# A hybrid transformer block on one core: the last feed-forward part in halves, identity products in planned waits, a first load by tiles, and new constants in the planner that orders the work

## The chip, the cores and the metric

The kernel runs on one core of one Trainium2 chip. A core has TensorE (PE: matrix products and transposes, results into eight PSUM banks), VectorE (DVE), ScalarE (ACT), GpSimd (POOL), the DMA engines, and SyncE (SP), which here issues most DMAs. The metric is the device time of one execution in microseconds (us). Before the change the median of three runs is 2589.13 us (2588.81 to 2591.01).

## The reference

The input is 16 sequences of 512 tokens by 256 channels, float32. Each sequence goes through four residual stages, each on its layer-normed input, called a, f, b and h in the kernel:

```
x = x + attn_a(norm(x))   # a: 16 heads of 16; keys within 32 tokens, or one of the
                          #    first 4 tokens as key or query; softmax; out projection
x = x + ffn(norm(x))      # f: 256 -> 768 twice, silu(gate) * up, 768 -> 256, int weights / 127
x = x + attn_b(norm(x))   # b: exp(rotated q.k) / sum(exp(unrotated q.k)), causal mask after
                          #    the division, times v; out projection
x = x + ffn(norm(x))      # h: the same weights as f
```

In b the denominator runs over all 512 keys, also those that the causal mask takes out of the numerator.

## The kernel before, in words

All weights lie in SBUF. A sequence `b` (0 to 15) is held as four tiles of 128 tokens (`xt`, tile index `t`), and its stages are Python generators that yield one operation at a time: `normalize` (L460), `window_attention` (a), `feed_forward` (f and h, L1032), `rotary_attention` (b), `products` (L1289), `load` and `store`. Per stage one sequence is in work at a time; different stages work on different sequences at once, so in steady state a of one sequence runs beside f, b and h of earlier ones.

The order of the instructions on every engine is written by a planner, `Plan` (L86), before the kernel is emitted. Every yielded operation carries an engine, an estimated time, the names that it needs, and the buffers that it takes and gives back. `Plan.run` repeatedly takes, from the operations that could start soonest, the one of lowest key, and emits it there; each engine executes its own list in that order, and semaphores hold an instruction until its inputs are there. The plan is made once.

On TensorE the key is the rank of the thread and then `progress` plus `turn`. Progress is the number of the sequence, plus a fixed lead of the stage (`LEAD`: a 0, f 0.885, b 1.59, h 2.77), plus the share of the stage that is done: it sets how far apart the stages run. `turn` is a price for changing the shape in which the 128x128 array is used. There are three shapes: FULL (all rows and columns; transposes, and in the profile `128*128`), COLS (four column strips of 32, `128*32`) and ROWS (four row strips of 32, the score products `dn`, `nm` and `sa`, `32*128` and `32*64`). Projections are FLEX: FULL when the array is in FULL, otherwise COLS. `TURN` has the price of each change, in sequences, and `hold`, the time for which an operation in ROWS is awaited when the array is in ROWS. On the other engines the key is: operations that give a buffer back first, then rank, then progress.

Names for the trace: `lt_*` are the transposes of a normed input, `xnt_*` the transposed copies, `psc_g*`/`psc_u*` gate and up products, `th_*` the tanh and silu product, `ht_*` the hidden layer, `po_*` a projection back to 256 channels. In a: `sa` scores, `sc` masked scores and weights, `tp` their transposes, `ya` the products with the values. In b: `dn` scores of the denominator, whose exponentials ACT sums (L1164); `nm` rotated scores, whose exponentials go to `ptb` (L1215), where POOL zeroes what is above the diagonal (L1225); `yb` the products with the values (L1309); `db` the inverse denominators, by which DVE multiplies `yb` (L1319).

`products` runs over ten groups, five for each half of the channels (`oc`), and sums a half's five groups in one bank; only after the fifth does DVE read the bank, for all 512 tokens. A half's third and fourth group end what tokens 0 to 255 need; the fifth holds keys 256 to 383 alone. The projection of b follows in four tiles of tokens, and each adds its result to `xt` (L547). `normalize` of stage h then takes statistics by tile (L471, L472), the inverse deviation of all four tiles at once on POOL (L475, L476), scales four tiles (L481) and transposes them; both halves of the transposed channels are copied out (L517, L519), and only then does the first gate product run. `xn` has one buffer, `ht` and the transposed input of f and h (`in_f`) one each.

The loads are issued at the top: sequence 0 in one DMA of 512 KB on SP (L273), then on the same queue `wk`, `wq`, `wv`, `wo` (L319), sequence 1, the three raw feed-forward weights (L330), `wqkv` and `wout`. `make_identity` writes the identity matrix `ident` with POOL.

Of the kernel before, what the change touches and what calls it, by code (L numbers as in the profile page):

```python
# [81 lines left out]
LAG = {"pe": 0.26, "act": 0.2, "dve": 0.2, "pool": 0.2, "sp": 0.1}  # L82
BORDER = {"fr": 0.30, "fc": 0.15, "rf": 0.21, "rc": 0.13, "cf": 0.21, "cr": 0.21}
NEVER = 1e9

class Plan:  # L86
# [3 lines left out]
    def __init__(self, slots):  # L90
        self.free = dict.fromkeys(LAG, 0.0)
        self.at = {}
        self.slots = {tag: [0.0] * n for tag, n in slots.items()}
        self.threads = []
        self.lying = FULL
        self.slow = 0.0
        self.sbuf = 0.0
        self.done = {}

# [3 lines left out]
    def ready(self, op):  # L103
# [3 lines left out]
        for tag in op.takes:  # L107
            if tag in ("u", "s"):
                at = max(at, sorted(self.slots["bank"])[0 if tag == "u" else 3])
            if tag != "s":  # L110
                at = max(at, min(self.slots[tag]))
# [8 lines left out]
    def take(self, op):  # L120

        for tag in op.takes:
            if tag == "s":
                op.k[tag] = [self.pick("bank") for _ in range(4)]
            elif tag == "u":
                op.k[tag] = self.pick(tag), self.pick("bank")
            else:
                op.k[tag] = self.pick(tag)
# [8 lines left out]
    def progress(self, thread):  # L137

        _, _, stage, seq, _ = thread
        return seq + LEAD[stage] + self.done.get((stage, seq), 0.0) / SHARE[stage]  # L140
# [14 lines left out]
    def run(self):  # L155
        while True:
# [4 lines left out]
            for t in self.threads:  # L161
# [9 lines left out]
                cand.append((start, t))  # L171
            assert cand, [(t[2], t[3], t[1].needs, t[1].takes) for t in self.threads]
# [17 lines left out]
            else:  # L190
                start, t = min(soon, key=lambda c: (not c[1][1].gives, c[1][4], self.progress(c[1])))
            op = t[1]
            us = op.us
            if engine == "pe":
                op.lying = self.lies(op)
# [26 lines left out]
TURN = {"hold": 0.05, "fr": 0.0, "fc": 0.3, "rf": 0.3, "cf": 1.0, "rc": 0.0, "cr": 0.15}  # L222
LEAD = {"a": 0.0, "f": 0.885, "b": 1.59, "h": 2.77}
# [3 lines left out]
def kernel(  # L227
# [43 lines left out]
    def load_x(b, k):  # L271
        t = work.tile([P, NT, D], F32, tag=f"x{k}", name=f"x_{b}")
        nc.sync.dma_start(t, x[b].rearrange("(t p) d -> p t d", p=P))  # L273
# [185 lines left out]

    def normalize(stage, b):  # L460

        me = f"{stage}{b}"
        needs = added(before[stage], b) if stage in before else [f"x{b}"] * NT
        slot = input_of[stage]
        for t in range(NT):
            op = yield dve(0, needs[t], us=0.51)
            if t == 0:
                xt = xs[b]
                stats = work.tile([P, NT, 6], F32, tag=f"stats_{stage}", name=f"stats_{me}")
                mv = work.tile([P, NT, 2], F32, tag=f"mv_{stage}", name=f"mv_{me}")  # L470
            nc.vector.bn_stats(stats[:, t, :], xt[:, t, :])  # L471
            nc.vector.bn_aggr(mv[:, t, :], stats[:, t, :])  # L472
        op = yield pool(0, op.end, us=1.6)
        rstd = work.tile([P, NT], F32, tag=f"rstd_{stage}", name=f"rstd_{me}")
        nc.gpsimd.tensor_scalar(rstd, mv[:, :, 1], EPS, None, ALU.add)  # L475
        nc.gpsimd.tensor_tensor(rstd, rstd, neg_half, ALU.pow)  # L476
        op = yield dve(0, op.end, us=1.5, takes=("xn", slot), sbuf=True)
        k_xn = op.k["xn"]
        xn = work.tile([P, NT, D], F32, tag="xn", name=f"xn_{me}")
        for t in range(NT):  # L480
            nc.vector.tensor_scalar(  # L481
                xn[:, t, :],
                xt[:, t, :],
                mv[:, t, 0:1],
                rstd[:, t : t + 1],
                ALU.subtract,
                ALU.mult,
            )
        there = op.end
        if stage in "ab":  # L490
            bias = bias_sb["bo" if stage == "a" else "bout"]

            def add_bias(op):
                nc.gpsimd.tensor_tensor(
                    xt, xt, bias.unsqueeze(1).to_broadcast([P, NT, D]), ALU.add
                )

            plan.start(
                one(pool(0, there, "bo", us=2.3, makes=f"bias_{me}", sbuf=True), add_bias), stage, b, 2
            )  # L500
        else:
            plan.at[f"bias_{me}"] = 0.0
        for c in range(NC):
            op = yield pe(
                0.44, there, takes=("u",), gives=(("xn", k_xn),) if c == NC - 1 else ()
            )
            ps = bank(op, [P, S], f"lt_{me}_{c}")
            for t in range(NT):
                nc.tensor.transpose(
                    ps[:, t * P : (t + 1) * P], xn[:, t, c * P : (c + 1) * P], ident  # L510
                )
            if c == 0:
                xnt[me] = work.tile([P, NC, S], F32, tag=slot, name=f"xnt_{me}")

            def keep(_, c=c, ps=ps):
                if c == 0:
                    nc.vector.tensor_copy(xnt[me][:, c, :], ps)  # L517
                else:
                    nc.scalar.copy(xnt[me][:, c, :], ps)  # L519

            how = dict(gives=(("u", op.k["u"]),), makes=f"xnt_{me}.{c}")
            plan.start(
                one(dve(S, op.end, **how) if c == 0 else act(S, op.end, **how), keep), stage, b, -1
            )
# [952 lines left out]
```

## Time and profile before

| | |
|---|---|
| median of three runs | 2589.13 us |
| the profiled execution | 2590.64 us |
| its span, first to last instruction | 2588.8 us |
| PE busy | 2540.2 us, 98% |
| DVE / ACT / POOL busy | 1560.9 / 1479.0 / 947.8 us |
| chain that ended last | PE 94%, DVE 2%, ACT 2% |
| mean granted TensorE clock | 0.993 |

The profile tells of one execution. Busy times are shares of the span; 40 digits cut the span into equal slices and give the busy share of an engine in tenths, and PEclk the TensorE clock that was granted, in tenths of full speed. A row of the timeline gives the start, the time, engine, line, operation, what it writes and reads, the shape, the count, and in brackets the idle time before it with what ended that. A row of the table by stretches gives, for a stretch of the span, the busy time and instructions of each engine, then the granted clock, the share of DMA time and GB/s.

### The profile page before, as it was taken

To read this page: it belongs to the slowest core of one execution; us is meant where nothing else is said; L and a number is where in the kernel's file an instruction comes from. 1 tells how busy PE (TensorE), PEld (TensorE's weight loads), DVE (VectorE), ACT (ScalarE), POOL (GpSimd) and SP (SyncE) were. 2 spreads that over 40 slices of the span, in tenths; PEclk is the share of its full clock that TensorE was granted. 3 is DMA by queue.
4 is the path that set the end of the run, shared out by engine and by line. 5 is a ranking of instruction groups with operands and counts; after the bars stand their busy time and mean duration, and the time that the engine had idled before them with its cause. 6 is when DMAs were issued, how large, how long until landed. Compare 5 with 4: busy or idle time off the path is not lost.

```text
span 2588.8 us, 79000 instructions
## 1 busy us (share of the span) xinstructions
PE 2540.2 (98%) x34928; PEld 1266.8 (49%) x34928; DVE 1560.9 (60%) x3046; ACT 1479.0 (57%) x3689; POOL 947.8 (37%) x963
## 2 busy tenths in 40 slices
PE   7899999999999999999999999999999999999998
PEld 4554445455454544545445453554545445454434
DVE  7854856557574665746558565575746657465332
ACT  3646574746647465474755647455474654647473
POOL 5612524144351533424244341443515344241201
PEclk9899999999999999999999999999999999999999
DMA  4100010000100001000000100001000010100000
GB/s 140 26 24 2 2 41 2 25 18 2 41 2 25 19 2 41 2 25 18 19 24 2 41 2 24 19 2 41 2 25 18 2 41 2 33 2 2 10 10 9
DMA packets 26680, 50.81 MB, mean 20 GB/s; under 512 B 2337, under 2 KB 21217, under 8 KB 26337
## 3 DMA queue, kind: packets, MB, share of 16 engines
q1 hardware_dynamic: 24976, 44.83, 6.1%
q8 instruction: 274, 4.49, 0.7%
q10 hardware_dynamic: 1360, 0.93, 0.1%
q14 instruction: 70, 0.57, 0.1%
HBM read 13.77 MB, written 8.39 MB: 9 GB/s over the span
## 4 chain that ended last, share of the span: by engine, by line
PE 94%; DVE 2%; ACT 2%; DMA 1%; POOL 1%; issue 0%; SPq 0%; POOLq 0%; ACTq 0%; DVEq 0%
PE dn L1183 11%; PE psc_gh L451 7%; PE nm L1249 7%; PE po_h L451 7%; PE psc_uh L451 7%; PE psc_uf L451 7%; PE psc_gf L451 6%; PE po_f L451 6%; PE yb L1309 5%; PE tp L866 4%; PE sa L737 3%; PE ya L924 2%; PE po_a L451 2%; PE psc_qb L451 2%; PE po_b L451 2%; PE psv_b L451 2%
## 5 line engine op out<-in xcount | busy, mean ns | idle before, releaser
L1164 ACT ACTIVATE dn<-dn 128x512 f32<-128x512 f32 x1024 | 599.4, 585 | 146.5 <-PE dn L1183 146.5
L1215 ACT ACTIVATE ptb<-nm 128x512 f32<-128x512 f32 x640 | 330.0, 606 | 276.0 <-PE nm L1249 275.9
L1183 PE MATMUL dn<-kt,qb 32*128 32x512 f32 x2048 | 302.7, 638 | 0.0
L1225 POOL TENSOR_SCALAR_AFFINE_SELECT ptb<-ptb 128x512 f32<-128x512 f32 x256 | 159.3, 634 | 384.7 <-ACT ptb L1215 384.7
L818 POOL TENSOR_TENSOR sc<-sc,sm 128x1056 f32<-128x1056 f32 x128 | 249.1, 1952 | 114.7 <-DVE sm L813 66.0
L803 POOL TENSOR_TENSOR sc<-sc,sm 128x1056 f32<-128x1056 f32 x120 | 232.6, 1952 | 140.8 <-DVE sm L785 129.3
L1164 ACT ACTIVATION_READ_ACCUMULATOR dn<-dn 128x1 f32 x1024 | 192.0, 187 | 0.0
L772 DVE TENSOR_TENSOR sc<-sa,mask 128x512 f32<-128x512 f32 x256 | 159.7, 680 | 51.1 <-PE sa L737 51.1
L1249 PE MATMUL nm<-qr,kr 32*128 32x512 f32 (+3 forms) x2048 | 189.6, 462 | 0.7 <-DVE sc L772 0.7
L451 PE MATMUL psc_gh<-xnt_h,wg_sb 128*32 128x512 f32 (+1 forms) x1452 | 189.4, 596 | 0.0
L1044 ACT ACTIVATE th_f<-psc_gf 128x512 f32<-128x512 f32 x96 | 57.8, 602 | 230.2 <-PE psc_gf L451 230.2
L451 PE MATMUL psc_uh<-xnt_h,wu_sb 128*32 128x512 f32 (+1 forms) x1308 | 183.4, 595 | 0.0
L451 PE MATMUL psc_uf<-xnt_f,wu_sb 128*32 128x512 f32 (+1 forms) x1476 | 183.1, 594 | 0.0
L451 PE MATMUL psc_gf<-xnt_f,wg_sb 128*32 128x512 f32 (+1 forms) x1476 | 182.8, 593 | 0.0
L451 PE MATMUL po_h<-wd_sb,ht_h 128*32 128x256 f32 (+1 forms) x1992 | 178.1, 381 | 0.2 <-ACT sc L810 0.2
L451 PE MATMUL po_f<-wd_sb,ht_f 128*32 128x256 f32 (+1 forms) x2856 | 177.7, 380 | 0.0
L1183 PEld LDWEIGHTS dn<-kt,qb 32*128 32x128 f32 x2048 | 87.8, 183 | 179.3 <-ACT dn L1164 76.0
L1309 PE MATMUL yb<-ptb,vb 128*32 128x512 f32 (+3 forms) x2048 | 169.7, 441 | 1.0 <-POOL ptb L1225 1.0
L812 DVE TENSOR_REDUCE sm<-sc 128x8 f32<-128x1056 f32 x120 | 148.3, 1236 | 19.4 <-ACT sc L810 19.2
L785 DVE TENSOR_REDUCE sm<-sc 128x8 f32<-128x1056 f32 x128 | 154.6, 1238 | 0.0
L601 POOL COPY rdcb<-rden 128x1024 f32<-128x1024 f32 x16 | 16.6, 1036 | 352.6 <-DVE rden L1264 352.6
L810 ACT ACTIVATE sc<-sc 128x1056 f32<-128x1056 f32 x120 | 128.8, 1090 | 29.2 <-POOL sc L803 27.4
(175 smaller groups left out, 4087.8 us busy)
## 6 DMA issues: line engine op xcount, KB each, us to landing
vw<-va SPq DMA_DIRECT2D x30, 576.0 KB, 5.5
x<-in_x_dram SPq DMA_DIRECT2D x16, 512.0 KB, 3.9
out_dram<-x SPq DMA_DIRECT2D x16, 512.0 KB, 3.0
vw<-va SPq DMA_DIRECT2D x30, 144.0 KB, 5.4
vw<-vb SPq DMA_DIRECT2D x2, 576.0 KB, 6.1
raw_wg_sb<-in_w_gate_dram SPq DMA_DIRECT2D x1, 768.0 KB, 8.9
raw_wu_sb<-in_w_up_dram SPq DMA_DIRECT2D x1, 768.0 KB, 10.3
raw_wd_sb<-in_w_down_dram SPq DMA_DIRECT2D x1, 768.0 KB, 11.4
```

The costliest lines, as they stand in the source:

```text
L451: nc.tensor.matmul(out[s], w[:, s], moving, skip_group_check=True, **how)
L772: nc.vector.tensor_tensor(flat[:, 4 * j : 4 * j + 4, 0:P], ps[j].rearrange("p c two w -> p (c two) w"), mask.unsqueeze(1).to_broadcast([P, ...
L785: nc.vector.tensor_reduce(small[:, 0, hs], part, AX.X, ALU.max, negate=True)
L803: nc.gpsimd.tensor_tensor(part, part, small[:, 0, hs].unsqueeze(2).to_broadcast([P, H // 2, P + NG]), ALU.add,)
L812: nc.vector.tensor_reduce(small[:, 1, hs], part, AX.X, ALU.add)
L818: nc.gpsimd.tensor_tensor(part, part, small[:, 1, hs].unsqueeze(2).to_broadcast([P, H // 2, P + NG]), ALU.mult,)
L1164: nc.scalar.activation(ps[j], ps[j], AF.Exp, scale=SCALE, accum_out=den[:, t, h : h + 1])
L1183: nc.tensor.matmul(ps[j], tiles["qb"][rows, par, oc, t * P : (t + 1) * P], tiles["kt"][rows, oc, :], start=True, stop=True,)
L1215: nc.scalar.activation(pt[:, j, :], ps[j], AF.Exp, scale=SCALE)
L1225: nc.gpsimd.affine_select(out=pt[:, :, at : at + P], in_=pt[:, :, at : at + P], pattern=[[0, 4], [1, P]], compare_op=ALU.is_ge, fill=0.0, ...
L1249: nc.tensor.matmul(ps[j][:, at : at + n], tiles["kr"][rows, oc, c * P : (c + 1) * P], tiles["qr"][rows, par, oc, c * P :], start=True, sto ...
L1309: nc.tensor.matmul(y_ps[rows, c * P :], vb[:, c, 4 * oc + j, par : par + 2, :], pt[:, j, at : at + n], start=len(seen) == 1, stop=len(seen ...
```

## The change

There are five parts.

1. Stage h of sequence 15 works in two halves of 256 tokens: norm, transposes, gate, up and down projections of tokens 0 to 255, then the same of tokens 256 to 511. For this, the second half of the channels of `products` of sequence 15 is summed in two banks, one for each half of the tokens; the first is read after the fourth group, the second after the fifth. `xn` and the inverse deviations are made for each half.
2. Where the planner expects TensorE to wait over 1.2 us (`FILL`), and a bank is free by then, it emits products of `ident` with `ident` (128x128, FULL) ahead of the waiting operation: (gap - 0.35) / 0.22 of them; for the very first wait (gap - 5) / 2 stands for the gap. The array counts as FULL afterwards. Their results are not read.
3. Sequence 0 is loaded in four DMAs of 128 KB, one for each tile of tokens, and its statistics wait for their own tile in the plan.
4. In the plan's first 110 us (`EARLY`), the engines other than TensorE take the lowest sequence first, ahead of the old key. A POOL operation that shares the SBUF port (`sbuf`) is planned after a VectorE one that could start at about the same time.
5. The constants are others: `TURN` (hold 0.05 to 0.15; FULL to COLS 0.3 to 0.15; ROWS to FULL 0.3 to 0.2; COLS to FULL 1.0 to 0.2; ROWS to COLS 0 to 0.05; COLS to ROWS 0.15 to 0.05), `LEAD` (f 0.727, b 1.333, h 2.645), and `ENDS`, which moves seven single stages of the first and last sequences.

```diff
+FILL = 1.2
+EARLY = {"us": 110.0}
...
             for tag in op.takes:
-            if tag in ("u", "s"):
-                at = max(at, sorted(self.slots["bank"])[0 if tag == "u" else 3])
+            n = {"uu": 2, "s": 4}.get(tag, 1)
+            if tag in ("u", "uu", "s"):
+                at = max(at, sorted(self.slots["bank"])[n - 1])
...
-        return seq + LEAD[stage] + self.done.get((stage, seq), 0.0) / SHARE[stage]
+        return seq + LEAD[stage] + ENDS.get(f"{stage}{seq}", 0.0) + self.done.get((stage, seq), 0.0) / SHARE[stage]
...
+            first = [c[0] for c in cand if c[1][1].sbuf and c[1][1].engine == "dve"]
+            if first:
+                least, us = min((c[0], c[1][1].us) for c in cand if c[1][1].sbuf and c[1][1].engine == "dve")
+                cand = [
+                    (least + us, t) if t[1].sbuf and t[1].engine == "pool" and least <= s <= least + us else (s, t)
+                    for s, t in cand
+                ]
...
-                start, t = min(soon, key=lambda c: (not c[1][1].gives, c[1][4], self.progress(c[1])))
+                start, t = min(
+                    soon,
+                    key=lambda c: (
+                        c[1][3] if least < EARLY["us"] else 0,
+                        not c[1][1].gives,
+                        c[1][4],
+                        self.progress(c[1]),
+                    ),
+                )
             op = t[1]
             us = op.us
             if engine == "pe":
+                gap = start - self.free["pe"]
+                if not self.free["pe"]:
+                    gap = (gap - 5.0) / 2
+                k = min(range(8), key=lambda k: self.slots["bank"][k])
+                if gap > FILL and self.fill and self.slots["bank"][k] <= self.free["pe"]:
+                    self.fill(k, int((gap - 0.35) / 0.22))
+                    self.lying = FULL
+                    self.free["pe"] = start
...
-TURN = {"hold": 0.05, "fr": 0.0, "fc": 0.3, "rf": 0.3, "cf": 1.0, "rc": 0.0, "cr": 0.15}
-LEAD = {"a": 0.0, "f": 0.885, "b": 1.59, "h": 2.77}
+TURN = {"hold": 0.15, "fr": 0, "fc": 0.15, "rf": 0.2, "cf": 0.2, "rc": 0.05, "cr": 0.05}
+LEAD = {"a": 0.0, "f": 0.727, "b": 1.333, "h": 2.645}
+ENDS = {"b0": -0.05, "b2": -0.29, "h0": -0.04, "a0": 0.57, "a1": -0.08, "f15": -0.26, "h13": -0.11}
...
-        nc.sync.dma_start(t, x[b].rearrange("(t p) d -> p t d", p=P))
+        src = x[b].rearrange("(t p) d -> p t d", p=P)
+        for part in [slice(i, i + 1) for i in range(NT)] if b == 0 else [slice(NT)]:
+            nc.sync.dma_start(t[:, part, :], src[:, part, :])
...
+    def parts_of(stage, b):
+        n = 2 if stage == "h" and b == B - 1 else 1
+        return [slice(S // n * i, S // n * (i + 1)) for i in range(n)]
...
...     # normalize: all of it inside
+        for n, tokens in enumerate(parts_of(stage, b)):
+            tiles = range(tokens.start // P, tokens.stop // P)
+            ts = slice(tiles.start, tiles.stop)
...
+            op = yield pool(0, op.end, us=1.6)
+            nc.gpsimd.tensor_scalar(rstd[:, ts], mv[:, ts, 1], EPS, None, ALU.add)
+            nc.gpsimd.tensor_tensor(rstd[:, ts], rstd[:, ts], neg_half[:, ts], ALU.pow)
+            takes = ("xn",) if n else ("xn", slot)
+            op = yield dve(0, op.end, us=0.375 * len(tiles), takes=takes, sbuf=True)
...
...     # feed_forward: gate, up and down projections inside
+        for n, tokens in enumerate(parts):
+            us = 1.72 / len(parts)
...
@@ products
+            parts = [slice(S)]
+            if b == B - 1 and oc == NC - 1:
+                parts = [slice(S // 2), slice(S // 2, S)]
+            first = i % each == 0
+            takes = ("u" * len(parts),) if first else ()
...
+                for part, (ps, _, seen) in zip(parts, y_ps):
+                    lo = max(c * P, part.start or 0)
+                    if lo >= part.stop:
+                        continue
...
@@ load
-        plan.at[f"x{b}"] = op.end + 5.0 if b > 1 else (5.5, 22.0)[b]
+        for t in range(NT):
+            there = op.end + 5.0 if b > 1 else 22.0 if b else 3.4 + 0.7 * t
+            plan.at[f"x{b}.{t}"] = there
...
+    def fill(k, n):
+        ps = psum.tile([P, P], F32, tag=f"bank{k}", name=f"fill_{len(filled)}")
+        filled.append(n)
+        for _ in range(n):
+            nc.tensor.matmul(ps, ident, ident, start=True, stop=True)
```

## The prediction

> **What bounds the kernel now.** I read the page first, then the table by stretches, then the timelines of the first 120 us and the last 110. The page:
>
> ```profile
> span 2588.8 us, 79000 instructions
> PE 2540.2 (98%) x34928; PEld 1266.8 (49%) x34928; DVE 1560.9 (60%) x3046; ACT 1479.0 (57%) x3689; POOL 947.8 (37%) x963
> PE   7899999999999999999999999999999999999998
> PEclk9899999999999999999999999999999999999999
> ```
>
> TensorE is the bound except at the ends: only the first two slices and the last are under 9. The table by stretches (busy time and instructions of PE, PEld, DVE, ACT, POOL; then clock, DMA share, GB/s):
>
> ```profile
> 0.00:100.00 100.00, 71.38 (x1301) 49.31 (x1301) 75.16 (x161) 45.08 (x144) 53.50 (x72) 0.90 0.33 101
> 100.00:200.00 100.00, 95.86 (x1149) 55.20 (x1151) 63.38 (x126) 49.98 (x142) 31.17 (x30) 1.00 0.08 21
> 200.00:300.00 100.00, 95.14 (x1469) 46.77 (x1458) 59.12 (x112) 60.05 (x144) 43.22 (x43) 0.97 0.01 2
> 300.00:400.00 100.00, 100.00 (x1365) 44.05 (x1367) 62.94 (x111) 67.06 (x175) 35.69 (x33) 1.00 0.10 27
> ```
> ```profile
> 2510.00:2520.00 10.00, 10.00 (x56) 5.06 (x49) 0.97 (x2) 10.00 (x31) 1.67 (x2) 0.82 0.15 52
> ...
> 2540.00:2550.00 10.00, 5.29 (x92) 2.43 (x88) 4.61 (x14) 0.57 (x2) 2.49 (x4) 1.00 0.01 2
> ```
>
> PE idles 28.6, 4.1 and 4.9 us in the first three hundreds, 37.6 in all, then hardly. From 2510 to 2520 it counts as busy, but so is ACT, PE runs only 56 instructions, and the clock falls to 0.82: PE stands before banks that ACT has yet to read.
>
> The head, in VectorE's own order:
>
> ```profile
> 51.30 2.96 DVE L481 TENSOR_SCALAR xn_a<-x,mv_a,rstd_a 128x256 f32<-128x256 f32 x4
> ...
> 56.25 0.42 DVE L471 BATCH_NORM_STATS2 stats_a<-x 128x6 f32<-128x256 f32 x1
> ...
> 59.84 2.47 DVE L772 TENSOR_TENSOR sc<-sa,mask 128x512 f32<-128x512 f32 x4
> ```
> ```profile
> 117.59 2.96 DVE L481 TENSOR_SCALAR xn_f<-x,mv_f,rstd_f 128x256 f32<-128x256 f32 x4
> ```
>
> The mask additions at 59.84 belong to sequence 0's third score tile, whose products ended on PE at 42.05. Meanwhile VectorE normed sequence 2 (51.30) and took statistics of sequence 3 (56.25). So f of sequence 0, which would feed PE, is normed only at 117.59.
>
> The tail, on PE, and ACT beside it:
>
> ```profile
> 2510.95 2.58 PE L1183 MATMUL dn<-kt,qb 32*128 32x512 f32 x16
> 2513.01 6.29 PE L1249 MATMUL nm<-qr,kr 32*128 32x512 f32 x16
> ...
> 2538.36 2.05 PE L1309 MATMUL yb<-ptb,vb 128*32 128x384 f32 x32
> 2541.38 1.23 PE L1309 MATMUL yb<-ptb,vb 128*32 128x256 f32 x16 [0.98 <-POOL ptb L1225]
> ...
> 2550.33 2.21 PE L509 MATMUL lt_h<-ident,xn_h 128*128 128x128 f32 x8 [3.60 <-DVE xn_h L481]
> 2552.46 2.66 PE L451 MATMUL psc_gh<-xnt_h,wg_sb 128*128 128x512 f32 x4
> ```
> ```profile
> 2524.28 16.29 ACT L1215 ACTIVATE ptb<-nm 128x512 f32<-128x512 f32 x32 [2.29 <-PE nm L1249]
> ```
>
> After 2511 only b of sequence 15 is left, and ACT's exponentials pace it (32 in a row to 2540.6). Then its last products, the projection, the norm and the transposes follow one upon the other; the first gate product of h starts at 2552.46.
>
> **Part 1, halves (T1).** Group four's products end at 2540.41. The first half of DVE's product with `db` takes 0.42 (a 128x256 addition, L547; 0.69 at 512): 2540.9. Two token tiles of the projection are half of 3.27 us (2543.49 to 2546.77), 1.64: 2542.6. Addition 0.42, statistics 0.43 and 0.18 for the second tile: 2543.7. From there to the first scaled tile the old chain took 1.48 (POOL 0.23 and 1.04, and hops): 2545.2. Two tiles of `xn` are half of 1.38: 2545.9. Two transposes and a 0.42 copy: about 1.0, so the gate product starts near 2546.9, 5.5 us earlier. Beside this PE does group five (1.0), a wait for its part of `db`, and the other two tiles (1.64), ending near 2545.8; so there is hardly a wait left, and the clock holds: gate at 1.88 instead of 2.66, 0.8 more. T1 is -6.3. If the plan puts group five ahead of the two tiles, its mask (2541.34) and 1.0 of products come first, 1.7 us, POOL's 1.48 may then be waited for twice, and the clock falls again: -2.3. With the cold transposes gone too (2.21 against 1.09 for eight `tp` at 60.32), -7.4. What halving adds is covered: 48 more gate and up products move the same columns (48 `po_h` of 256 took 10.37, 0.216 each, half of 0.43); two 128x256 operations on DVE, 0.84, stand under 1.72 of PE for each of six blocks; POOL's second 1.3 and DVE's second 0.7 lie under 10.3 us of first-half gate and up. Some 32 more `yb` records cost 0 to 0.3. The end stays: the last addition, then one DMA, 4.4 us after the last product.
>
> **Part 5, the last stages placed apart (T2).** Ten groups of `nm` at 1.07, ten of `yb` at 1.0, `dbp` 1.0 and the last `dn` 1.9 are 24 us of PE's rows, and they stretch from 2510.95 to 2542.4, 31.5: 7.5 could hold other work. Just before, 11 us of `po_h` of sequence 14 (2496.3 to 2511) ran while ACT was busy 7.46 of 10. The new leads put h 1.31 behind b instead of 1.18, and f of 15 is drawn 0.26 ahead, so some of h 14 can move beside the exponentials. I take half, -4; bounds -8 and +3, for `ht` and `in_f` have one buffer, and a late h 14 holds up h 15.
>
> **Part 5, the middle (M).** A change of shape has a price: eight `dn` between two blocks take 1.07 (2481.83 to 2482.90), sixteen 1.93, so the second eight take 0.86 and entering costs 0.21; sixteen `psc` take 1.85 after `dn` and 1.74 after `psc`, 0.11. Mean 0.16. Counted over PE's rows from 300 to 2440 us the shape changes 864 times, about 140 us of 2140. The new prices pull both ways: a longer hold and an end to the price of 1.0 for COLS to FULL save detours, a round trip ROWS-COLS-ROWS at 0.10 instead of 0.15 and cheaper FULL invite more. Nothing in the trace decides; I take 0 and bounds of 10% of the changes, 86 x 0.16, -14 and +14. The Trainium skill, "TensorEngine Tiling (Array Packing)", section Tiling Modes, Key Properties, says that a change of tiling mode drains the engine; it speaks against cheaper turns, and by it alone M would be above 0, by 7 us for 5% more.
>
> **Part 4, sequence first (H).** DVE's rows from 42.05 to 59.84 that are not sequence 0's (`qa` 3.0, `va` copies 0.8, `xn_a` 3.0, statistics 2.2, `xnt` 0.7) are 9.7 us, and between 110.95 and 117.59 there are 6.2 of `L785`, `qa` and `va`. If all went behind sequence 0, its f came 16 us earlier; the second lot lies at the edge of 110 us, and a of sequences 1 and 2 is late instead. I take half, -8; bounds -19 (half of the 37.6 idle) and +6 (the second lot, turned against us where b of 0 and f of 1 starve at 180 and 250 us).
>
> **Part 3 (X).** Statistics start at 4.95, when 512 KB have landed, and end at 7.18. By tiles three may be done before the last lands: -1, at best -1.7 (three of 0.57). Against it, three more issues at 0.44 push `wk`, `wq`, `wv`, sequence 1 and the raw weights on SP's queue by 1.3 us; `wo` landed about 10.3 and is used at 11.7, so it is the next late one. DVE waits for raw weights at 16.66 and 18.66 while the DMA engines are at 0.90 to 1.06 of their time, so bytes rather than issues time those. Worst +1.3. Behind the statistics that wait for a tile DVE has nothing else before `xn_a` at 9.15.
>
> **Part 2 (C).** Clock lost in stretches is 1.0 (25 to 30), 2.4, 1.7, 0.4 and 4.7 (80 to 90 at 0.53), 10.2 in the head, 3.0 in 200 to 300: 13.2 at most, while PE is seldom the bound there. I take -2. The waits over 1.2 us sum to about 25 without the first, (25 - 12 x 0.35) / 0.22, some 95 products; at 0.11 (a `tp`) all in the way would cost 10. But they stand in a wait, half as long as it when warm, and hurt only where the real wait is under half of the planned one: +3. A fill writes a bank whose reader should be done; if DVE or ACT is late there, all of PE's queue stands behind it. Ends -6 (half of 13.2) and +3. The rows show what wait costs clock: 3.05 us before `sgp` at 27.41 are followed by 0.80 and 0.76, and the ten around 1.70 us at 65.68 have 0.83. The Trainium skill, "TensorE: Matmul & The Clock Gate", Part 1, has the clock halve after an idle window of about 3.4 us; by that alone only two inner waits (3.80, 3.60) would need filling, an estimated 1.7 each from that page, and C and the clock in T1 would be -3.4 together.
>
> **Sum.** -6.3 - 4 + 0 - 8 - 1 - 2, and 0.3 for records: -21. The profiled run took 2590.64, its span 2588.8 with 1.8 around; the median, 2589.1, is 1.5 lower. I subtract from the median: 2568.
>
> **Rivals.** (A) The forecast, 2557 to 2580: H off by half of the way to an end (6), T2 likewise (3), C by 2. (B) Only the halves pay: eight blocks of exponentials on ACT (L792, 16.3% of the chain in the first 130 us) pace the head whichever sequence goes first, and h 14 stays where it was: -6.3 - 1, 2582. For it: that share; against: the 9.7 us of others' work. (C) Turns fall by 10% as well: -21 - 14, 2554. For it: the detours at 1.0 vanish. (D) Slower: cheaper turns make so many more that they eat the gain. From 21 / 0.16, 131 more (15%), it is level; at 20% (173, 28 us) 2596. For it: 140 us hang on this count, and three prices fell; against: ROWS work comes as ACT frees banks, whatever the price. The fills may not be there at all (in the tail `nm` and `yb` hold most banks): 2570, within A.
>
> **How the numbers follow.** A 0.52, B 0.18, C 0.15, D 0.15. What a measurement tells from no change is 0.2%, 5.2 us: 2583.9 to 2594.3. Faster: A, C and 0.11 of B, 0.78; same: 0.07 of B and 0.02 of D, 0.09; slower 0.13. The range runs from 2548, C with H another 6 nearer its far end, to 2591, where D has eaten the gain and 2 us more; A's own is above.
>
> **What would show it.** T1: two sizes of `yb` for sequence 15, the first h gate within 7 us of the last `ptb` mask, clock 1.00 from then. T2: `psc_gh` or `po_h` between the last `nm`. H: the third tile's additions before 50 us, `xn_f` before 112, over 75 busy in the first 100. C: `fill` rows, 80 to 90 above 0.53. M: changes of shape in the middle within 10% of 864. I am wrong if PE idles elsewhere after 300 us, if the count rises by 15%, or if f of sequence 0 starts no earlier.

## The result, and the profile after

The changed kernel takes 2567.86 us (median of six runs, 2566.33 to 2569.0), the kernel before, run beside it, 2588.97. The ratio is 0.9916, 95% interval 0.9904 to 0.9929: 21 us less, where 21 were forecast. The profiled execution has a span of 2567.3 us (before 2588.8).

The page of the changed kernel, then its table by stretches (columns as in the prediction):

```profile
span 2567.3 us, 79967 instructions
PE 2536.9 (99%) x35384; PEld 1278.3 (50%) x35384; DVE 1543.8 (60%) x3060; ACT 1481.6 (58%) x3696; POOL 949.8 (37%) x965
PE   8999999999999999999999999999999999999999
PEclk9999999999999999999999999999999999999999
```
```profile
0.00:100.00 100.00, 86.64 (x1501) 62.58 (x1502) 84.06 (x181) 49.09 (x154) 59.70 (x78) 0.97 0.35 107
100.00:200.00 100.00, 98.61 (x1070) 48.00 (x1072) 54.42 (x110) 60.08 (x180) 26.22 (x24) 1.00 0.06 16
200.00:300.00 100.00, 98.08 (x1483) 48.99 (x1475) 63.13 (x123) 62.95 (x149) 45.48 (x44) 0.97 0.01 2
300.00:400.00 100.00, 99.94 (x1380) 44.50 (x1383) 49.42 (x96) 60.33 (x145) 32.98 (x38) 1.00 0.10 27
```

VectorE has 84.06 in the first hundred (before 75.16), as order by sequence should give. TensorE's idle time in the first three hundreds is 16.7 us (before 37.6), but 11.2 us of PE's busy time there are identity products whose results nobody reads, so 27.9 are not spent on the task.

**Where the time came from.** A total says nothing about the place. I added up, over PE's rows in order of time, the time that each product's columns need when nothing holds it up (0.43 us for 512 columns at the full clock, a quarter of it where four strips run side by side), the identity products left out; all of the kernels reach the same 2331.8 us of such work. The moment at which two kernels have the same amount behind them shows how far one is ahead of the other:

| streamed work, us | 60 | 100 | 250 | 600 | 1200 | 2220 | 2290 | 2330 |
|---|---|---|---|---|---|---|---|---|
| kernel before is there at, us | 105.5 | 148.4 | 328.3 | 705.1 | 1350.9 | 2449.4 | 2533.6 | 2582.3 |
| changed kernel, us earlier | 10.8 | 11.8 | 16.9 | 12.8 | 12.2 | 16.9 | 20.0 | 21.6 |

So the head (to 328 us) gives 16.9, the 2100 us of middle give nothing on balance (4.7 lost by 1351, won again by 2449), and the tail 4.7. The forecast had 11 for the head (H, X, C), 0 for the middle (M) and 10.3 for the tail (T1, T2). That the total came out as forecast is luck: the head was 5.9 better and the tail 5.6 worse than forecast.

PE's idle time from 300 to 2440 us rises from 0.7 to 8.2 us. The prediction named "if PE idles elsewhere after 300 us" as a sign of being wrong: it came, in small, and 4.1 us of it lie where the middle loses its 4.7, 3.9 where it wins them again.

The head, in VectorE's order of the changed kernel:

```profile
45.80 2.47 DVE L823 TENSOR_TENSOR sc<-sa,mask 128x512 f32<-128x512 f32 x4
...
97.98 1.39 DVE L526 TENSOR_SCALAR xn_f<-x,mv_f,rstd_f 128x256 f32<-128x256 f32 x4
```

The mask additions of sequence 0's third score tile run at 45.80 instead of 59.84, and f of sequence 0 is normed at 97.98 instead of 117.59: 19.6 us earlier.

The tail on PE, from group four on:

```profile
2520.28 1.07 PE L1375 MATMUL yb<-ptb,vb 128*32 128x128 f32 x24 [0.62 <-POOL ptb L1283]
2521.28 1.60 PE L1452 MATMUL fill<-ident 128*128 128x128 f32 x12
2522.82 1.07 PE L1375 MATMUL yb<-ptb,vb 128*32 128x256 f32 x16
2523.70 3.64 PE L486 MATMUL po_b<-wout_sb,db 128*32 128x256 f32 x64
2527.27 2.72 PE L1452 MATMUL fill<-ident 128*128 128x128 f32 x22
2530.05 0.66 PE L560 MATMUL lt_h<-ident,xn_h 128*128 128x128 f32 x4
2531.01 1.13 PE L486 MATMUL psc_gh<-xnt_h,wg_sb 128*128 128x256 f32 x4 [0.30 <-DVE xnt_h L568]
```

And VectorE's product with `db` for the first half of the tokens:

```profile
2520.82 0.42 DVE L1384 TENSOR_TENSOR db<-yb,db 128x256 f32<-128x256 f32 x1 [6.80 <-PE yb L1375]
```

The first half of `db` is there by 2521.2. (PE's ends are modelled: VectorE reads group four's sums from 2520.82, before the row of group four ends.) PE nevertheless runs 12 identity products, then group five, and only then (2523.70) all four tiles of the projection, 64 products in one block. The first gate product starts 9.66 us after group four's end (2521.35 to 2531.01), before it was 12.05 (2540.41 to 2552.46): 2.4 won instead of 5.5.

### The profile page after: what moved, and what is told of

Same layout as the page of the kernel before. It is cut to its first block, busy times and chain, and to the rows that moved or that the text cites. A ratio compares the mean times of both kernels' runs of the same rounds, so it can differ in the third digit from the quotient of the medians.

```text
span 2567.3 us, 79967 instructions
## 1 busy us (share of the span) xinstructions
PE 2536.9 (99%) x35384; PEld 1278.3 (50%) x35384; DVE 1543.8 (60%) x3060; ACT 1481.6 (58%) x3696; POOL 949.8 (37%) x965
## 4 chain that ended last, share of the span: by engine, by line
PE 80%; DVE 15%; POOL 3%; issue 1%; ACT 1%; DMA 0%; SPq 0%; DVEq 0%; POOLq 0%
PE dn L1241 9%; PE po_h L486 7%; PE psc_gf L486 7%; PE psc_uf L486 7%; PE nm L1307 7%; PE po_f L486 6%; PE psc_uh L486 6%; PE yb L1375 5%; PE psc_gh L486 5%; DVE sm L836 3%; DVE sc L823 2%; PE psc_ka L486 2%; PE tp L917 2%; PE psv_a L486 2%; PE psc_qa L486 2%; DVE sm L863 2%
## 5 line engine op out<-in xcount | busy, mean ns | idle before, releaser
L1241 PE MATMUL dn<-kt,qb 32*128 32x512 f32 x2048 | 288.9, 634 | 0.3 <-DVE vb L629 0.2
L486 PE MATMUL po_h<-wd_sb,ht_h 128*32 128x256 f32 (+1 forms) x2496 | 186.4, 381 | 1.2 <-issue 1.2
L486 PE MATMUL psc_uh<-xnt_h,wu_sb 128*32 128x512 f32 (+2 forms) x1188 | 184.0, 586 | 2.0 <-DVE th_h L1098 1.8
L1307 PE MATMUL nm<-qr,kr 32*128 32x512 f32 (+3 forms) x2048 | 183.2, 459 | 1.2 <-issue 1.2
L486 PE MATMUL psc_gh<-xnt_h,wg_sb 128*32 128x512 f32 (+2 forms) x1200 | 183.5, 585 | 0.5 <-DVE xnt_h L568 0.3
L1375 PE MATMUL yb<-ptb,vb 128*32 128x256 f32 (+3 forms) x2080 | 164.1, 431 | 0.6 <-POOL ptb L1283 0.6
L1098 DVE SCALAR_TENSOR_TENSOR th_f<-th_f,psc_gf 128x512 f32<-128x512 f32 x96 | 65.5, 683 | 156.5 <-ACT th_f L1096 156.3
L1307 PEld LDWEIGHTS nm<-qr,kr 32*128 32x128 f32 x2048 | 93.2, 184 | 104.1 <-issue 62.7
```

The source lines that it names most:

```text
L486: nc.tensor.matmul(out[s], w[:, s], moving, skip_group_check=True, **how)
L1241: nc.tensor.matmul(ps[j], tiles["qb"][rows, par, oc, t * P : (t + 1) * P], tiles["kt"][rows, oc, :], start=True, stop=True,)
L1307: nc.tensor.matmul(ps[j][:, at : at + n], tiles["kr"][rows, oc, c * P : (c + 1) * P], tiles["qr"][rows, par, oc, c * P :], start=True, sto ...
L1375: nc.tensor.matmul(ps[rows, lo : part.stop], vb[:, c, 4 * oc + j, par : par + 2, :], pt[:, j, at + lo - c * P : at + part.stop - c * P], s ...
```

## The experiments

"Earlier" and "later" below are against the kernel before at equal streamed work, as in the table.

**1. Halves alone (part 1).** All other parts undone.

```diff
 (against the changed kernel)
-EARLY = {"us": 110.0}
+EARLY = {"us": 0.0}
-            if first:
+            if False:
...   TURN, LEAD as before, ENDS empty, x[0] in one DMA
-    plan.fill = fill
```

> The kernel before with the halves of stage h and the two banks alone: old constants, no identity products, one load, old order on the other engines. As predicted (the first two token tiles projected ahead of group five): the first h gate starts 6 us after group four's products instead of 12, 2583 us. If the projection stays behind group five, as one generator yields both: the gate starts 9 to 10 us after group four, and the time is 2586 to 2588.

Measured: 2589.31 us, ratio 0.9999 (0.9989 to 1.0008). PE's timeline and the stretches of 5 us around it:

```profile
2540.06 1.08 PE L1375 MATMUL yb<-ptb,vb 128*32 128x128 f32 x24 [0.62 <-POOL ptb L1283]
2542.14 1.23 PE L1375 MATMUL yb<-ptb,vb 128*32 128x256 f32 x16 [1.00 <-POOL ptb L1283]
...
2549.72 1.57 PE L486 MATMUL psc_gh<-xnt_h,wg_sb 128*128 128x256 f32 x4 [0.84 <-DVE xnt_h L568]
...
2551.98 1.87 PE L486 MATMUL psc_uh<-xnt_h,wu_sb 128*128 128x256 f32 x4
```
```profile
2545.00:2550.00 5.00, 2.88 (x41) 1.56 (x34) 4.05 (x14) 0.37 (x1) 1.43 (x4) 1.00 0.00 0
2550.00:2555.00 5.00, 5.00 (x19) 3.90 (x19) 1.91 (x5) 1.01 (x3) 0.46 (x1) 0.66 0.00 0
```

The gate starts 8.6 us after group four, 3.45 better than before. But group four itself ends 0.7 later, and from the gate to the end of the span it takes 37.9 us instead of 36.3: the clock falls to 0.66 just as the gate products begin, which take 1.57 and 1.87 where later ones take 1.03. What is left is 1.2 us of span, too little for the medians to show. The gate starts a little earlier after group four than the second expectation has it, but the time lies above both ranges: neither had the cold clock at the gate. With the projection behind group five, halves alone are worth about 1 us.

**2. Two tiles of the projection ahead of group five.** The changed kernel, with the generator of `products` yielding the projection of tiles 0 and 1 before the last group.

```diff
+        def project(tiles):
+            for t in tiles:
+                yield from project_out("b", b, t, ...)
         for i, (oc, segments) in enumerate(groups):
+            if b == B - 1 and i == len(groups) - 1:
+                yield from project(range(NT // 2))
...
-        for t in range(NT):
-            yield from project_out(...)
+        yield from project(range(NT // 2 if b == B - 1 else 0, NT))
```

> The changed kernel with the projection of token tiles 0 and 1 of sequence 15 yielded ahead of the fifth group of products. If the order inside the generator cost the missing part of T1: the first h gate starts 6 to 7 us after group four instead of 9.7, and the time is 2563 to 2565. If VectorE and GpSimd pace the norm whichever comes first: gate at 9 or more, 2567 to 2568.

Measured: 2564.94 us, ratio 0.9903 (0.9889 to 0.9918), span 2565.3 against 2567.3. PE's timeline:

```profile
2520.76 1.07 PE L1392 MATMUL yb<-ptb,vb 128*32 128x128 f32 x24 [0.62 <-POOL ptb L1283]
2521.65 1.91 PE L486 MATMUL po_b<-wout_sb,db 128*32 128x256 f32 x32
2523.37 1.05 PE L1392 MATMUL yb<-ptb,vb 128*32 128x256 f32 x16
...
2525.57 1.99 PE L486 MATMUL po_b<-wout_sb,db 128*128 128x256 f32 x8
2527.54 0.87 PE L560 MATMUL lt_h<-ident,xn_h 128*128 128x128 f32 x4
2529.05 1.13 PE L486 MATMUL psc_gh<-xnt_h,wg_sb 128*128 128x256 f32 x4 [0.64 <-DVE xnt_h L568]
```

Now the order is the one that T1 was worked out for, and the gate starts 7.2 us after group four (2521.83 to 2529.05); the working had 6.5. This settles what T1 missed: the order within the generator. The medians differ by 2.9 us, the spans by 2.0.

**3. The last result stored in halves as well.** A DMA for each half of the tokens.

```diff
-        op = yield Op("sp", 0.3, *added("h", b))
-        nc.sync.dma_start(out[b].rearrange("(t p) d -> p t d", p=P), xs[b])
+        for part in parts_of("h", b):
+            ts = slice(part.start // P, part.stop // P)
+            op = yield Op("sp", 0.3, *added("h", b)[ts])
+            dst = out[b].rearrange("(t p) d -> p t d", p=P)
+            nc.sync.dma_start(dst[:, ts, :], xs[b][:, ts, :])
```

> The changed kernel with token tiles 0 and 1 of sequence 15 projected ahead of group five, and its result stored in two halves, the first while the second is computed. The first part measured 2564.9. The last transfer shrinks from 512 to 256 KB: the 4.5 us after the last product become 3.3 to 4, 2563.5 to 2564.5. If the fixed part of a transfer rules (128 KB took 2.4 us to land against 3.9 for 512): no more than 0.5 less.

Measured: 2564.62 us, ratio 0.9905 (0.989 to 0.9919). DMA issues in the last microseconds (KB each, us from issue to landing), of the changed kernel and of this one:

```profile
out_dram<-x SPq DMA_DIRECT2D x1, 512.0 KB, 2.9
```
```profile
out_dram<-x SPq DMA_DIRECT2D x1, 256.0 KB, 2.1
```

The stretch after the last product shrinks from 4.48 to 3.58 us. The span shows 0.8 of it against experiment 2, the medians 0.3, within their spread.

**4. Order by sequence alone (part 4).** Everything else undone, and of part 4 only `EARLY` kept, without the rule for POOL's operations.

```diff
 (against the kernel before)
+EARLY = {"us": 110.0}
...
+                        c[1][3] if least < EARLY["us"] else 0,
```

> The kernel before with sequence-first order alone (first 110 us of the plan), old constants, no identity products, one load, no halves. If this order is what the head gained by: feed-forward norm of sequence 0 near 105 instead of 117.6, and 2575 to 2582 if the middle keeps it. If the constants are needed to keep it, the first sequences after 300 us give it back: 2586 to 2600 with the norm early all the same. If the order gained nothing by itself: norm at 115 or later.

Measured: 2581.25 us, ratio 0.997 (0.9958 to 0.9982). VectorE's row of f of sequence 0:

```profile
101.37 1.37 DVE L526 TENSOR_SCALAR xn_f<-x,mv_f,rstd_f 128x256 f32<-128x256 f32 x4
```

It is normed 16.2 us earlier than before. The work is 11.9 us earlier at 200 us of it, 10.0 at 600, 9.8 at 2220 and 8.7 at the end: the head's gain is carried through 2100 us of a full TensorE almost whole. H was put at -8.

**5. No order by sequence in the changed kernel.**

```diff
-EARLY = {"us": 110.0}
+EARLY = {"us": 0.0}
```

> The changed kernel with sequence-first order off from the start (110 us made 0), all else as changed. If the order by sequence made the head faster: the third score tile of sequence 0 waits again for the norms of later sequences, its additions come after 55 us and its feed-forward norm after 110, and the time is 2577 to 2584. If the new constants and the fills made the head faster, the feed-forward norm of sequence 0 stays near 98 us and the time is 2567 to 2571.

Measured: 2598.16 us, ratio 1.0032 (1.0021 to 1.0043), 30 us above the changed kernel and outside both ranges. The additions come at 57.85 and f of sequence 0 is normed at 105.57, the first after 55 as expected, the second not after 110. Only 14 of the 30 us are lost in the head (3.0 earlier at 200 us of work instead of 17.2). Between 250 and 600 us of work it goes from 1.3 earlier to 18.3 later, with waits of 1.56, 1.26 and 0.92 us (the changed kernel has one of 1.57 there), which explain only part of it. The rest is not shown; another head makes another plan of the stages behind it.

**6. No identity products planned (part 2).**

```diff
-    plan.fill = fill
```

> The changed kernel without identity products. If they are worth what the prediction gave them (2 us, PE being seldom the bound in the head): 2568 to 2572, with stretches of the first 100 us below a clock of 0.9. If the clock made the head faster: 2576 to 2582. If they stand in the way of PE (48 of them from 34.9 to 40.5): 2563 to 2566.

Measured: 2592.01 us, ratio 1.001 (1.0 to 1.0019), 24 us above the changed kernel and outside all three ranges. But the head is only 3.0 worse (13.9 earlier at 250 us of work); the rest goes between 250 and 1200, in part in waits of 0.8 to 1.6 us before eight different operations. That looks like a large effect of the products. It is not, as the next run shows.

**7. The same plan, the products not emitted.** The planner still does its bookkeeping (array counted as FULL, the wait as filled), but nothing is put into PE's queue.

```diff
-    plan.fill = fill
+    plan.fill = lambda k, n: None
```

> The changed kernel with the plan and so every engine's order kept as it is, the 148 identity products alone not emitted. What differs is then only the clock and what the products hold up. If the clock was worth what the fills were drawn for: the first 100 us fall under 0.9 in several stretches, sequence 0's feed-forward norm comes 3 to 8 us later, and the time is 2571 to 2576. If the 24 us of the run without fills came from the other plan alone: 2567 to 2570.

Measured: 2567.69 us, ratio 0.9915 (0.99 to 0.993), against 2567.86 with the products. First its first hundred, then PE's tail:

```profile
0.00:100.00 100.00, 73.07 (x1268) 51.25 (x1269) 83.12 (x168) 47.91 (x149) 56.85 (x75) 0.95 0.35 106
```
```profile
2520.92 1.23 PE L1375 MATMUL yb<-ptb,vb 128*32 128x256 f32 x16 [1.00 <-POOL ptb L1283]
2521.97 3.64 PE L486 MATMUL po_b<-wout_sb,db 128*32 128x256 f32 x64
2526.88 0.78 PE L560 MATMUL lt_h<-ident,xn_h 128*128 128x128 f32 x4 [1.28 <-DVE xn_h L526]
2528.50 1.59 PE L486 MATMUL psc_gh<-xnt_h,wg_sb 128*128 128x256 f32 x4 [0.84 <-DVE xnt_h L568]
```

In the head f of sequence 0 is normed 4.9 us later, at 102.90, as the first expectation has it, and the work is 5 us behind the changed kernel's at 60 to 100 us of it; but at 200 it is level (0.3). In the tail it reaches the gate 2.5 us earlier, as no product stands before group five and the transposes, and then loses most of that to a colder clock (gate 1.59 instead of 1.13); the spans differ by 0.8. The 148 products are worth nothing on balance; the 24 us of experiment 6 belong to the different plan that comes out when the planner no longer reckons with them.

**8. All old constants (part 5 undone).**

```diff
-TURN = {"hold": 0.15, "fr": 0, "fc": 0.15, "rf": 0.2, "cf": 0.2, "rc": 0.05, "cr": 0.05}
-LEAD = {"a": 0.0, "f": 0.727, "b": 1.333, "h": 2.645}
+TURN = {"hold": 0.05, "fr": 0.0, "fc": 0.3, "rf": 0.3, "cf": 1.0, "rc": 0.0, "cr": 0.15}
+LEAD = {"a": 0.0, "f": 0.885, "b": 1.59, "h": 2.77}
...
+ENDS = {}
```

> The changed kernel with the turn prices and leads of before and no single stages moved; halves, identity products, sequence-first order and loads by tiles stay. If the constants only placed the last stages (T2): the head is as in the changed kernel, the tail from 2 to 3 us longer, 2569 to 2573. If the constants are what lets the middle keep the head's gain: 2580 to 2595, lost between 300 and 1000 us.

Measured: 2596.8 us, ratio 1.003 (1.002 to 1.004). At 250 us of work it is 10.1 earlier, as order by sequence alone is (10.5), so the head's other 6.8 us come from the constants. At 2290 it is 6.6 later. The time lies just above the second range, and the loss is not where that put it: 6.0 goes between 250 and 600 us of work, 1.0 to 1200, and 10.2 between 1200 and 2220. PE's groups from 1280 to 2230 us, six sequences, name the wait (columns: count, busy us, mean ns, idle before and who ended it):

```profile
L917 PE MATMUL tp<-ident,sc 128*128 128x128 f32 x384 | 48.0, 276 | 8.2 <-DVE qa L660 8.2
```

1.36 us in each sequence, with others 2.08. The same constants in the kernel before, and with order by sequence alone, leave no such wait in the middle. Against order by sequence alone (2581.25) this kernel has the halves, the planned products, the loads by tiles and the rule for POOL's operations more: in the head these bring nothing together (10.1 against 10.5), and which of them makes the wait in the middle no run tells.

**9. One group of constants undone at a time.** Three kernels, each the changed one with the old `TURN`, with the old `LEAD`, or with `ENDS = {}`.

> The changed kernel with the old prices of a change of shape (TURN) alone. Theory 1, the new prices make the middle's shorter period (156.06 us and 61.0 changes of shape per sequence, before 156.77 and 63.2): the period from sequence 8 to 14 goes back to about 156.8, the count from 300 to 2440 us above 855, the time +4 to +8, 2572 to 2576. Theory 2, the ordered parts fit only each other: whichever constant is undone, the stages fall into another pattern with waits that come back, and the time goes up by 15 or more, above 2583. Rival D of the prediction, cheaper turns cost time by themselves: the old prices would then be faster, below 2563.

> The changed kernel with the old leads of the stages (LEAD), the new prices and shifts kept. Theory 1, the leads make the period shorter, and the new prices do little: the period from sequence 8 to 14 near 156.8 and the time +4 to +8, 2572 to 2576. Theory 2, the parts fit only each other: a wait recurs in every period, as with all old constants (0.4 before a gate product and 1.4 before a transpose of a, 2.1 us per sequence), 2585 or more. Rival: worth nothing, 2566 to 2570.

> The changed kernel without the seven shifts of single stages (ENDS empty). Theory 1, they are worth only what they move at the two ends, the head's 6 us beyond the order by sequence and the 2 of the last stages: 2570 to 2577, with the middle's period as it was, 156.1. Theory 2, they set the phase in which the stages meet for the whole run: waits of 1 us and more between 300 and 1300 us, 2585 or more. Rival: worth nothing, 2566 to 2570.

Measured, with the middle counted over the six sequences from the eighth's f on, changes of shape as in the prediction, idle time in waits over 0.15 us:

| | time, us | ratio (95%) | earlier at 250 / 2290 us of work | us per sequence | changes of shape | PE idle, us per sequence |
|---|---|---|---|---|---|---|
| before | 2588.97 | | 0 / 0 | 156.77 | 63.0 | 0.0 |
| changed | 2567.86 | 0.9916 (0.9904 to 0.9929) | 16.9 / 20.0 | 156.06 | 60.8 | 0.1 |
| old `TURN` | 2641.59 | 1.02 (1.0184 to 1.0215) | 12.6 / -53.7 | 161.12 | 56.2 | 3.17 |
| old `LEAD` | 2602.75 | 1.0049 (1.0034 to 1.0064) | 19.2 / -15.3 | 159.22 | 60.5 | 1.08 |
| no `ENDS` | 2662.86 | 1.0287 (1.027 to 1.0304) | 7.8 / -72.2 | 162.28 | 58.5 | 2.87 |
| all old | 2596.8 | 1.003 (1.002 to 1.004) | 10.1 / -6.6 | 157.49 | 59.0 | 2.08 |

PE's groups of the middle with their idle time, of the kernel with the old `TURN`, with the old `LEAD` and without `ENDS`:

```profile
L486 PE MATMUL psc_gh<-xnt_h,wg_sb 128*128 128x512 f32 x68 | 36.1, 657 | 10.1 <-DVE xnt_h L568 10.1
```
```profile
L1241 PE MATMUL dn<-kt,qb 32*128 32x512 f32 x768 | 111.6, 632 | 3.1 <-DVE qb L660 3.1
```
```profile
L486 PE MATMUL psc_gh<-xnt_h,wg_sb 128*32 128x512 f32 x448 | 56.1, 606 | 5.5 <-DVE vb L629 5.1 <-issue 0.3
```

Each of the three is worse than all old together. The theory that one group makes the shorter period and costs 4 to 8 us when it goes has fallen; that the parts fit only each other holds. With the old `TURN` PE waits 1.68 us in every sequence for VectorE's copy of `xnt_h`, and in the planned waits there it puts 8.3 identity products per sequence. Seven shifts of stages, all of sequences 0 to 2 or 13 and 15, cost 95 us when they go, 83 of them between 250 and 2290 us of work. A wait of 1.56 us before `lt_b` comes at 438.0, 921.6, 1409.4, 1897.6 and 2381.1, so every three sequences, and others recur likewise: the stages settle into a beat early and keep it. The idle time explains 3.1 of the 5.1 us per sequence (old `TURN`), 1.0 of 3.2 (old `LEAD`) and 2.8 of 6.2 (no `ENDS`); the identity products emitted there are about 1.1 more with the old `TURN` (8.3 at 0.133, the 12 in 1.60 above) and 0.8 with the old `LEAD` (6.0 per sequence). The rest lies in time that PE counts as busy; where is open.

**10. All that helped together.** Experiments 2 and 3, with the products planned and not emitted.

```diff
 (against experiment 3)
-    plan.fill = fill
+    plan.fill = lambda k, n: None
```

> The changed kernel with the projection of the first two token tiles of sequence 15 yielded ahead of group five, the last result stored in two halves, and the identity products planned but not emitted, so that the plan is that of the changed kernel and PE's queue holds no product that is not read. If the products cost nothing and gain nothing, it takes the same as with them, 2564 to 2565. If they stand in the way in the tail by the 1.6 us that they take before group five, 2562.5 to 2563.5. If the clock that they keep up in the tail matters more, 2566 to 2567.

Measured: 2563.94 us (2562.3 to 2565.68), ratio 0.9901 (0.9886 to 0.9915). It is the fastest of all by its median, 3.9 below the changed kernel; against experiment 3 it is 0.7, inside the spread of both, so whether the products before group five cost anything stays open. Its gate runs at 1.13 without any product to keep the clock up: no wait in its tail is longer than 0.64.

## Why the prediction was right, and where not

**T1 (halves, -6.3; measured -2.4).** Its mechanism holds, but the step "Beside this PE does group five (1.0), a wait for its part of `db`, and the other two tiles" took for granted that the first two tiles of the projection go ahead of group five. The alternative was priced in the same place at -2.3, and it is what happened; the gate starts 8.1 us after the last mask ends, where the prediction wanted 7 (in experiment 2 it is 5.7). No plan had to decide it: in `products` the loop over the tiles follows the loop over the groups in one generator, and a generator yields in its own order. Experiment 2 turns it round, and wins 2.4 of the gate's 3.1 still missing. The 0.8 for the clock is not there either: the first gate products take 1.13 and are warm, yet from it to the end of the span the changed kernel takes 36.3 us as the one before does. Some 0.4 of that is the second half's four transposes, which now stand behind the gate (2533.70 to 2534.14); the rest is open.

**T2 (last stages apart, -4; measured -2.2).** Group four ends 19.1 us earlier than before, when the work was 16.9 ahead at 2449; the difference is 2.2. The prediction asked for `psc_gh` or `po_h` between the last `nm`. One block of 48 `po_h` is there, and nothing of h after it; from 2500 to 2520 the rows hold 15.1 us of products, while ACT is busy 18.6, so the exponentials still set the pace. The clock holds at 1.00 there (before 0.82 from 2510 to 2520):

```profile
2497.15 2.80 PE L486 MATMUL po_h<-wd_sb,ht_h 128*32 128x256 f32 x48
```
```profile
2510.00:2520.00 10.00, 9.66 (x145) 5.00 (x144) 0.69 (x1) 8.99 (x19) 4.12 (x7) 1.00 0.01 2
```

So the step that failed is "I take half, -4": one block of `po_h`, 2.8 us, is all the work of h that came in between, and the leads do not matter. From 2220 us of work to the end of group four the changed kernel gains 2.2 on the one before, and 2.2 as well with the old `LEAD`; with the old `TURN` 0.3, and without `ENDS` it loses 2.4. It is the shifts of single stages, with the prices, that gain here, and not h being 1.31 behind b.

**H (sequence first, -8; measured -8 to -10).** Right in place and in what the order does: additions at 45.80, f of 0 at 97.98; by itself 7.9 us by the medians, 9.8 at equal work where the middle ends. But the gain is only in part the idle time that H was drawn from: with order by sequence alone PE's idle time in the first 300 us falls by 4.8 (37.6 to 32.8), and the clock lost there from 13.7 to 6.8, so up to 6.9 may be clock, which H did not price. What it left out is that the constants reach into the head. They bring the other 6.8 us of the 16.9, of which nothing was forecast; taking away `ENDS` alone costs 9.1 there. And an early f of 0 does not make the head fast by itself: without `ENDS` it comes earliest of all, and that head is only 7.8 ahead at 250 us of work.

```profile
87.23 1.37 DVE L526 TENSOR_SCALAR xn_f<-x,mv_f,rstd_f 128x256 f32<-128x256 f32 x4
```

**X (load by tiles, -1; measured 0).** The three first tiles' statistics are done by 4.90, but the fourth waits for its DMA until 6.35, and POOL is at its mask until 7.66, so the inverse deviations start at 7.75, before at 7.76. VectorE in the changed kernel:

```profile
6.35 0.43 DVE L516 BATCH_NORM_STATS2 stats_a<-x 128x6 f32<-128x256 f32 x1 [1.45 <-DMA x<-in_x_dram]
...
9.14 1.38 DVE L526 TENSOR_SCALAR xn_a<-x,mv_a,rstd_a 128x256 f32<-128x256 f32 x4 [2.14 <-POOL rstd_a L520]
```

The step that failed is "three may be done before the last lands: -1": it asked what VectorE would save, not who is next. POOL was, and the timeline of before had its rows. Nor did the last tile land as early as the whole had: at 6.33, where all 512 KB were there at 4.93. Experiment 7 shows that POOL decides: there the fourth tile's statistics are done by 6.12, and the inverse deviations start no earlier.

```profile
7.75 0.23 POOL L519 TENSOR_SCALAR rstd_a<-mv_a 128x4 f32<-128x4 f32 x1
```

**C (identity products, -2; measured 0).** The clock lost in the first 300 us went from 13.7 to 6.8, as hoped, but it goes to 5.1 in the same plan without a single product emitted, and to 6.8 with order by sequence alone. So the term counted a gain that order by sequence makes already. By the page "TensorE: Matmul & The Clock Gate", Part 1, of the Trainium skill alone, C and the clock in T1 were put at -3.4 together; the runs show nothing of that either.

**M (middle, 0; measured 0).** The count went from 864 to 842, and the period shrank by 0.71 us, of which 2.2 changes at 0.16 are half. But the bounds of 14 were worked out from the count alone, and the count is not what decides: all kernels of experiment 9 change shape less often and are slower. With the old `TURN` there are 4.6 fewer per sequence, worth 0.7 us, and 3.07 more idle. This was the prediction's thinnest step; 0 came true, but with one group of constants otherwise the middle loses 34 to 80 us against the kernel before.

**The rivals.** B (only the halves pay) is refuted by experiment 4, since H alone gives 8 us. C needed 10% fewer changes, there were 2.5%. D (cheaper turns make more of them) has its sign right beside the new leads, 60.8 against 56.2, but 4.6 more of them at 0.16 are a seventh of the 5.1 us per sequence that the old prices cost. A's time held, though not its parts. Two pieces of the change were in no run alone: the rule that plans POOL's operations behind VectorE's, and the load by tiles.

## What to carry to other kernels

Work that is written as one generator, loop or queue keeps its own order: before pricing a part that becomes available earlier, look for the statement that lets it be used earlier. When the order is planned, a part cannot be valued by taking it out of the finished kernel, as that values another plan as well (24 us for products worth nothing): keep the plan and take out the instructions, or add the part to the kernel before. And a gain in the head of a pipeline that is full afterwards was kept here almost whole where no wait came back in every period (10.5 us at 250 us of work, 9.8 at 2220, order by sequence alone) and lost many times over where one did; so look for recurring waits per period before counting anything else.

## What the runs showed that was not expected

- Short waits in a row lower the clock as a long one does. In the kernel with halves alone no wait on PE from 2540 to 2550 is over 1.28 us, PE is busy 2.88 of the 5 us to 2550, and the next 5 us are granted 0.66; before, one wait of 3.60 stood there. The Trainium skill, "TensorE: Matmul & The Clock Gate", Part 1, speaks of an idle window of about 3.4 us; here 5 us that were 58% busy were enough. Over which stretch the clock is decided the runs do not show.
- From 200 to 300 us the changed kernel is granted 0.97 and the same plan without products 1.00. The changed kernel runs no identity product between 73 and 320 us, so this says nothing of the products; why the clock falls in one alone is open.
- The 512 KB store takes 2.9 us from issue to landing, a 256 KB store 2.1.
